# A graph stack of four attention layers: seven key blocks of the third layer turned by VectorE in the second, with masks fetched by quarters of the partitions

## The chip, the cores and the metric

The kernel runs on one core of a Trainium2 chip. The metric is the device time in microseconds from the start to the end of one execution; lower is better. The core has a matrix engine (TensorE, PE in the profile; its weight loads are PEld), a vector engine (VectorE, DVE), a scalar engine (ScalarE, ACT), GpSimd (POOL) and SyncE (SP), which here only issues transfers. GpSimd computes and issues transfers, both from one queue of instructions.

## The reference

Four graph attention layers over the same N = 4096 nodes and one adjacency matrix, D = 256 features. Each layer is followed by a residual sum and a layer norm. Cut to what matters:

```python
# layer 0: additive attention, 4 heads, softmax over j where adj; then elu
# layer 1: multi-head attention, 4 heads, scores q.k/8 + (adj.T - 1) * 10000
# layer 2: additive attention, one head
h = x @ W
e = leaky_relu((h @ a[:D])[:, None] + (h @ a[D:])[None, :], 0.01)
attention = softmax(where(adj > 0, e, -1e12), axis=1)
x = layernorm(x + elu(attention @ h))
# layer 3: cosine attention, rows of Wq x and Wk x normalised, mixed half and half with x
```

In the text they are called the first to the fourth layer. The change concerns how the third layer gets its operand `x @ W` and in which order it keeps the keys.

## The kernel before

The features X lie in SBUF for the whole run as 32 tiles of 128 nodes, `X[:, t, :]`. Every attention layer walks over 8 blocks of 512 queries (`NB`, `QW`), and inside a block over tiles of keys: 32 tiles of 128 in the first, third and fourth layer, 64 tiles of 64 in the second. One pair of block and key tile is called a unit. The layers follow one another at about 725, 1710 and 2213 us of the span.

*Second layer* (`multi_head_attention`, L536). Its main loop has an order written out by hand for TensorE, VectorE and ScalarE. A unit is: score matmuls (L664), an exponential on ScalarE (L666), the product with the mask on VectorE (L676), sums of the denominators on GpSimd (L683) and by accumulating transfers from GpSimd (L689), and the sums with V on TensorE (L697). `finish(b, j)` spreads the rest of a block over the units of the next: at step j of block b + 1 it joins denominators, turns results, and normalises rows of X; its last step was j = 41, when all four tiles of block b of X are final. For the last block, `tail` does this inside the third layer.

*Third layer* (`additive_one`, L401). A softmax weight factors into a term of the query (`src`) and a term of the key (`dst`), so a unit is one ScalarE instruction `e` (L456: relu of a row of query terms scaled by the key's), one VectorE instruction `prob` (L458: product with the mask) and four matmuls per query block into `acc` (L464, 8 records in the profile). Three buffers hold `prob`, four hold `mask`.

Before keys can be used, `x @ W` (`V`, with `src` and `dst` in its last columns) is made block by block: `turn(b)` transposes the four tiles of X on TensorE (`transposed_block`, 8 transposes at L118) and copies them out of PSUM on VectorE and ScalarE (L120); `project(b)` multiplies with W (L196), and ScalarE and VectorE write `src`, `dst` and `V` (L200 to L203). Blocks 0 and 1 are turned before the first unit; blocks 2 to 7 in the course of query block 0, `turn` at units 0, 4, ..., 20 and `project` two units later. After each `project`, `fill_row(b)` spreads `src` as a row over all partitions: for blocks 0 and 1 by TensorE (L446, L447), for the others by two transfers from GpSimd's queue, one to DRAM (`far`, L441) and one back to all partitions (`row`, L442), the second of which waits for the first at the head of the queue.

The order of TensorE in the third layer is written out by hand; a scheduler places the instructions of the other engines. The mask of two key tiles is one 512 KB transfer on SP's queue (L454), issued when the buffer is free.

*The end of the third layer.* `follow` (class `Cosine`) prepares the fourth layer within block 7 of the third: `prepare(b, step)` turns X by the other way. `turned_apart` (L123) makes two VectorE transposes of 32x32 squares (L131), stores the 512 KB in DRAM (`far`, L133) and fetches them by four 128 KB transfers, one for each quarter of 32 partitions (L135), so that a full turn comes out, with the keys of the block in another order. Step 0 does so for X on SP's queue, step 1 projects (L869) and normalises rows, step 2 turns these rows with `turned_apart` on GpSimd's queue (for six blocks) into `T`. GpSimd also fetches masks of the fourth layer (L854). L912 are the scores of the fourth layer, L920 its sums.

Of the kernel before, what the change touches and what calls it, by code (L numbers as in the profile page):

```python
# [9 lines left out]
FP = mybir.dt.float32  # L10
# [8 lines left out]
P = 128  # L19
D = 256  # L20
KC = D // P
QB = 4
QW = QB * P
# [5 lines left out]
def kernel(  # L29
# [49 lines left out]
    X = feat.tile([P, NT, D + 1], FP, name="X")  # L79
# [40 lines left out]
            copies[c](xT[:, c, :], pt)  # L120
        return xT.rearrange("p c (k i) -> p c k i", i=P)

    def turned_apart(squares, far, part, to, eng):  # L123

        B = P // QB
        squares = squares.tile([P, QB, KC, P], FP, name="squares")
        far = far.tile([QB, B, QB, KC * P], FP, name="far")
        for c in range(KC):  # L130
            nc.vector.transpose(squares[:, :, c, :].rearrange("p q (k n) -> p k q n", n=B),  # L131
                                part(c).rearrange("p k (q f) -> p k q f", f=B))
        eng.dma_start(far.rearrange("a f q m -> (a f) (q m)"), squares.rearrange("p q c m -> p (q c m)"))  # L133
        for q in range(QB):
            eng.dma_start(to[q * B:(q + 1) * B], far[:, :, q, :].rearrange("a f m -> f a m"))  # L135
        return to.rearrange("p a (c m) -> p c a m", c=KC)

    def block_apart(sb, once, dr, b, eng):
        xT = sb.tile([P, KC * QW], FP, name="xT").rearrange("p (a m) -> p a m", a=QB)
        return turned_apart(once, dr, lambda c: X[:, b * QB:(b + 1) * QB, c * P:(c + 1) * P], xT, eng)  # L140

    def one_row(mv, k, y):
        st = fin.tile([P, 6], FP, name="bn")
# [29 lines left out]
    def scale_row(y, mv, r, k):  # L173
        nc.vector.tensor_scalar(y, y, mv[:, k, 0:1], r[:, k:k + 1], OP.subtract, OP.mult)
# [226 lines left out]
    def additive_one(w_sb, slope, tail, op, follow):  # L401

        MJ = 2
        mvs, taken = {}, {}
        with ExitStack() as lay:
            keep = pool(lay, "gb_keep", 1)
            V = keep.tile([P, NT, D + 1], FP, name="V")
            src = keep.tile([P, NT, 1], FP, name="src")
# [1 line left out]
            row = keep.tile([P, N], FP, name="row")  # L410
            zp = pool(lay, "gb_z", 3)
            sb = pool(lay, "gb_sb", 2)
            xp = pool(lay, "gb_turn", 3)
            sq = pool(lay, "gb_squares", 1)
            far = pool(lay, "gb_far", 2, space=bass.MemoryType.DRAM)

# [2 lines left out]
            dr = pool(lay, "gb_dram", 2, space=bass.MemoryType.DRAM)  # L419

            ps = pool(lay, "gb_ps", 4, space=PSUM)
            pa = pool(lay, "gb_pa", 1, space=PSUM)
            edges = adjT.rearrange("(t p) i -> p t i", p=P)
            mask, acc, prob = {}, {}, {}

# [3 lines left out]
            def turn(b):  # L429
                return transposed_block(xp, bank, b)  # L430

            def project(b, xT, ks=range(QB)):
                groups = [(k, 1, bank().rearrange("p (n f) -> p n f", n=1)) for k in ks]
                additive_values(xT, b, groups, w_sb, V, src, dst, 1, slope)

            def fill_row(b):
                part = row[:, b * QW:(b + 1) * QW]
                if b > 1:

                    far = dr.tile([QB, P], FP, name="far")  # L440
                    nc.gpsimd.dma_start(far.rearrange("k p -> p k"), src[:, b * QB:(b + 1) * QB, 0])  # L441
                    nc.gpsimd.dma_start(part, far.rearrange("k p -> (k p)").unsqueeze(0).to_broadcast([P, QW]))  # L442
                    return
                pr = bank()
                for k in range(QB):
                    nc.tensor.transpose(pr[:, k * P:(k + 1) * P], src[:, b * QB + k, :].to_broadcast([P, P]), ident)  # L446
                nc.scalar.copy(part, pr)  # L447

            def weights(b, j):
                cols = slice(b * QW, (b + 1) * QW)  # L450
                m = b, j // MJ
                if j % MJ == 0:
                    mask[m] = mp.tile([P, MJ, QW], I32, name="mask")
                    nc.sync.dma_start(mask[m], edges[:, j:j + MJ, cols])  # L454
                e = sb.tile([P, QW], FP, name="e")
                nc.scalar.activation(e, row[:, cols], AF.Relu, bias=-1.0, scale=dst[:, j, :])  # L456
                prob[b, j] = zp.tile([P, QW], FP, name="prob")
                nc.vector.scalar_tensor_tensor(prob[b, j], e, 1.0, mask[m][:, j % MJ, :], OP.add, OP.mult)  # L458
# [26 lines left out]
            even = itertools.count()  # L485
            units = [(b, j) for b in range(NB) for j in range(NT)]
            with tc.manual_schedule(engines={mybir.EngineType.PE}):
                xTs = {0: turn(0), 1: turn(1)}
                project(0, xTs[0])
                project(1, xTs[1], [0, 1])  # L490
                fill_row(0)
                project(1, xTs[1], [2, 3])
                for i in range(len(units) + 1):
                    if i < len(units):
                        b, j = units[i]
                        weights(b, j)

                        if b == 0 and j // QB + 2 < NB:
                            n = j // QB + 2
                            if j % QB == 0:  # L500
                                xTs[n] = turn(n)
                            elif j % QB == 2:
                                project(n, xTs[n])
                                fill_row(n)
                    if i:
                        b, j = units[i - 1]
                        sums(b, j)
                        if (b, j) == (0, 1):
# [27 lines left out]
    def multi_head_attention(w_sb, b_sb, tail, rows_of_den, narrow_edges):  # L536
# [8 lines left out]
        MJ = 4  # L545
# [3 lines left out]
        with ExitStack() as lay:  # L549
# [91 lines left out]

            zp = pool(lay, "mh_z", 8)
            mp = pool(lay, "mh_mask", 3)
            ps = pool(lay, "mh_pz", 3, space=PSUM)
            pa = pool(lay, "mh_pa", 1, space=PSUM)
            mask, acc, prob, score = {}, {}, {}, {}
# [112 lines left out]
            def finish(b, j):  # L759

                rows = [X[:, b * QB + k, :D] for k in range(QB)]
                if j in (7, 9):
                    join_sums(b, j // 2 - 2)
                elif j == 12:
                    row_sums(halves(), b)
                elif j == 15:
                    bank = halves()
                    pd = turned_row_sums(bank, b)
                    po = turned_half(bank, b, 0)
                    reciprocals(pd, b)  # L770
                    half(po, b, 0)
                elif j == 18:
                    half(turned_half(halves(), b, 2), b, 2)
                elif j in (21, 23, 25, 27):
                    k = (j - 21) // 2
                    if k == 0:
                        mvs[b] = fin.tile([P, QB, 2], FP, name="mv")
                    one_row(mvs[b], k, rows[k])
                elif j == 29:
                    roots[b] = begin_root(mvs[b])  # L780
                elif j == 31:

                    end_root(*roots[b], nc.gpsimd)
                elif j in (35, 37, 39, 41):
                    k = (j - 35) // 2
                    scale_row(rows[k], mvs[b], roots[b][1], k)

# [40 lines left out]
    class Cosine:  # L828

        MJ = 4  # L830
# [192 lines left out]
        return part[:, t:t + QB, :]  # L1023

    w2_sb = const.tile([P, KC, D + 2], FP, name="w2_sb")
    wm_sb, bm_sb = {}, {}
    with ExitStack() as weights1, ExitStack() as den1, ExitStack() as weights3:
        wp = weights1.enter_context(tc.tile_pool(name="w1", bufs=1, side="right"))
# [66 lines left out]
```

## Time and profile before

The times of three runs and the profiled execution:

| | us |
|---|---|
| median of three runs | 2892.49 (2891.81 to 2894.18) |
| profiled execution | 2892.62 |
| its span | 2890.8 |
| TensorE busy in the span | 2879.6 |
| third layer on TensorE | 1710.2 to 2212.9 |
| its query block 0 | 1710.2 to 1803.8 |
| its query block 7 | 2136.9 to 2212.9 |

The granted clock of TensorE was 0.999 of full speed over the span. GpSimd's groups in the third layer's block 0, with mean durations of one instruction:

| group | instructions | mean ns |
|---|---|---|
| L441 `far<-src`, POOL issue | 6 | 775 |
| L442 `row<-far`, POOL issue | 6 | 546 |
| L706 denominators of the last block, POOL | 2 | 2601 |

How to read it: a row of a timeline is a run of like instructions on one engine, with its start and length, and in brackets the idle time before it and what ended it. The length of a matmul includes its way through the pipeline, so rows overlap a little; the difference of two starts is what a group costs. A transfer's issue on an engine's queue is short; when it lands is another matter, and an instruction that waits for the landing holds up its whole queue.

### The profile page before, as it was taken

Reading aid. Unit: us, or ns where it says so; the run is one execution under the profiler, and the core shown is the slowest. Engines: PE = TensorE matmul, PEld = TensorE weight load, DVE = VectorE, ACT = ScalarE, POOL = GpSimd, SP = SyncE. Lnnn points to the kernel's source line nnn. Section 1 sums busy time; section 2 is a strip of 40 time slices with the busy share of each in tenths; the row PEclk is TensorE's granted clock in tenths of the full one; section 3 lists DMA queues with packets and bytes.
Section 4 is the critical chain, followed back from the end, with each engine's and each line's share of the span. In section 5 each row is a group of like instructions: output and inputs, shape, how many; then the busy total and the mean of one; then the engine's idle time right before and its main releaser. Section 6 shows DMA issues by size and latency. Waiting matters only on the chain.

```text
span 2890.8 us, 50566 instructions
## 1 busy us (share of the span) xinstructions
PE 2879.6 (100%) x20093; PEld 1548.7 (54%) x20093; DVE 1959.5 (68%) x2557; ACT 1652.8 (57%) x2582; POOL 945.9 (33%) x705
## 2 busy tenths in 40 slices
PE   9999999999999999999999999999999999999999
PEld 4333333333543333333333358888888777777776
DVE  8899999998777777777777765655667323333333
ACT  7899999997356666666666653444444222222222
POOL 0010010100068988989899870000002000000000
PEclk9999999999999999999999999999999999999999
DMA  7566667675269989889899885565566434333441
GB/s 206 103 139 137 142 134 145 138 133 92 88 138 192 183 187 196 181 187 190 182 193 188 181 178 133 164 184 158 159 185 178 76 57 58 59 58 59 59 59 30
DMA packets 237087, 398.04 MB, mean 138 GB/s; under 512 B 20929, under 2 KB 121265, under 8 KB 235954
## 3 DMA queue, kind: packets, MB, share of 16 engines
q0 software_dynamic: 104320, 184.06, 40.1%
q1 hardware_dynamic: 132112, 210.36, 23.7%
q8 instruction: 157, 2.57, 0.3%
q14 instruction: 80, 0.66, 0.1%
q10 hardware_dynamic: 418, 0.40, 0.0%
HBM read 328.60 MB, written 32.58 MB: 125 GB/s over the span
## 4 chain that ended last, share of the span: by engine, by line
PE 99%; DVE 1%; ACT 0%; DMA 0%; issue 0%; SPq 0%; DVEq 0%
PE acc L293 23%; PE acc L920 15%; PE acc L697 15%; PE p L664 15%; PE acc L464 8%; PE g L464 8%; PE p L912 4%; PE g L912 3%; PE g L579 2%; PE g L196 1%; PE pv L598 1%; PE acc L869 1%; PE acc L196 1%; PE g L118 1%; PE g L305 0%; PE p L734 0%
## 5 line engine op out<-in xcount | busy, mean ns | idle before, releaser
L676 DVE TENSOR_TENSOR prob<-p,mask 128x1024 f32<-128x1024 f32 x512 | 624.0, 1223 | 209.4 <-ACT p L666 203.6
L666 ACT ACTIVATE p<-p,shift 128x1024 f32<-128x1024 f32 x512 | 556.2, 1088 | 325.2 <-PE p L664 324.4
L293 PE MATMUL acc<-prob,V 128*32 128x512 f32 x6144 | 664.0, 593 | 1.1 <-DVE prob L283 1.1
L683 POOL TENSOR_TENSOR den<-den,prob 128x1024 f32<-128x1024 f32 x248 | 626.4, 2526 | 73.9 <-DVE prob L676 66.6
L280 ACT ACTIVATE prob<-row,dst 128x512 f32<-128x512 f32 x1020 | 633.1, 712 | 0.1
L283 DVE SCALAR_TENSOR_TENSOR prob<-prob,mask 128x2048 f32<-128x2048 f32 x256 | 582.7, 2287 | 24.2 <-ACT prob L280 21.3
L664 PE MATMUL p<-qT,kT 64*64 64x512 f32 x4096 | 532.7, 590 | 0.8 <-DVE prob L676 0.8
L697 PE MATMUL acc<-prob,V 64*64 64x512 f32 x4096 | 531.8, 590 | 0.0
L920 PE MATMUL acc<-X,prob 128*128 128x257 f32 x2048 | 485.4, 380 | 0.0
L920 PEld LDWEIGHTS acc<-X,prob 128*128 128x128 f32 x2048 | 389.2, 190 | 161.6 <-issue 112.3
L917 DVE TENSOR_TENSOR prob<-prob,mask 128x512 f32<-128x512 f32 x256 | 176.7, 690 | 405.6 <-ACT prob L916 405.4
L293 PEld LDWEIGHTS acc<-prob,V 128*32 128x32 f32 x6144 | 197.8, 110 | 452.6 <-issue 431.9
L91 POOL COPY tick<-prob 128x1 f32<-128x1 f32 x35 | 40.2, 1150 | 996.0 <-DVE prob L283 644.5
L456 ACT ACTIVATE e<-row,dst 128x512 f32<-128x512 f32 x256 | 184.1, 721 | 241.7 <-DVE prob L458 212.7
L697 PEld LDWEIGHTS acc<-prob,V 64*64 64x64 f32 x4096 | 156.0, 133 | 285.2 <-issue 277.9
L664 PEld LDWEIGHTS p<-qT,kT 64*64 64x64 f32 x4096 | 154.6, 133 | 277.2 <-issue 261.4
L458 DVE SCALAR_TENSOR_TENSOR prob<-e,mask 128x512 f32<-128x512 f32 x256 | 175.5, 686 | 169.8 <-PE acc L464 92.4
L854 POOL DMA_DIRECT2D mask<-in_adjT x64 | 48.1, 751 | 585.2 <-DVE prob L917 523.6
L689 POOL DMA_DIRECT2D den<-prob x240 | 233.2, 972 | 15.7 <-DVE prob L676 6.7
L916 ACT ACTIVATE prob<-p 128x512 f32<-128x512 f32 x144 | 85.7, 596 | 258.4 <-PE p L912 244.3
L464 PE MATMUL acc<-V,prob 128*128 128x257 f32 x1024 | 225.1, 380 | 0.0
L464 PE MATMUL g<-V,prob 128*128 128x257 f32 x1024 | 223.7, 380 | 0.0
(165 smaller groups left out, 1937.1 us busy)
## 6 DMA issues: line engine op xcount, KB each, us to landing
mask<-in_adjT SPq DMA_DIRECT2D x256, 512.0 KB
den<-prob POOLq DMA_DIRECT2D x240, 512.0 KB, 5.1
mask<-edges SPq DMA_DIRECT2D x512, 64.0 KB
mask<-in_adjT POOLq DMA_DIRECT2D x64, 512.0 KB, 5.7
edges<-in_adj POOLq DMA_DIRECT2D x32, 512.0 KB, 9.8
far<-squares SPq DMA_DIRECT2D x16, 512.0 KB
den<-prob SPq DMA_DIRECT2D x16, 512.0 KB
row<-far SPq DMA_DIRECT2D x7, 1024.0 KB
```

The source lines that it names most:

```text
L280: nc.scalar.activation(z[:, h, :], r, AF.Relu, bias=-1.0, scale=dst[:, j, h:h + 1])
L283: nc.vector.scalar_tensor_tensor(z, z, 1.0, mask[m][:, j % MJ, :].unsqueeze(1).to_broadcast([P, H, QW]), OP.add, OP.mult)
L293: nc.tensor.matmul(acc[b][h * G:(h + 1) * G, n, :], part, prob[b, j][:, h, :], start=(j == 0), stop=(j == NT - 1))
L464: nc.tensor.matmul(acc[b][k][:, :D + 1], prob[b, j][:, k * P:(k + 1) * P], V[:, j, :], start=(j == 0), stop=(j == NT - 1))
L664: nc.tensor.matmul(p[c * d:(c + 1) * d, r, :], kT[half, c, at:at + d], qT[half, c, cols], start=True, stop=True)
L666: nc.scalar.activation(p, p, AF.Exp, bias=shift)
L676: nc.vector.tensor_tensor(z, p, mask[m][:, j % MJ, :].unsqueeze(1).to_broadcast([P, KC, QW]), OP.mult)
L683: nc.gpsimd.tensor_tensor(to, to, flat, OP.add)
L689: nc.gpsimd.dma_start(to, flat, accum_op=OP.add)
L697: nc.tensor.matmul(acc[b][c][r * d:(r + 1) * d, :], V[half, j, r * d:(r + 1) * d], prob[b, j][half, r, :], start=(j == 0), stop=(j == NH - 1))
L912: nc.tensor.matmul(p.rearrange("p (k i) -> p k i", k=QB), T[j // QB][:, 0, j % QB], T[b][:, 1], start=True, stop=True)
L920: nc.tensor.matmul(acc[b][k], prob[b, j][:, k * P:(k + 1) * P], X[:, j, :], start=(j == 0), stop=(j == NT - 1))
```

## The change

In the second layer, `finish` gets a step at j = 44: `squares_of` transposes the 32x32 squares of block b of X on VectorE (two instructions) and stores them in DRAM on SP's queue, for b = 0 to 6. In the third layer `fetch(b)` takes the place of `turn(b)` for these seven blocks: four transfers on SP's queue bring the squares to `xT`. Block 7, which is final only inside the third layer, is still turned by TensorE. Three blocks are fetched ahead instead of two turned.

The keys of a turned block come out in another order: key tile a of the block holds the nodes k x 128 + a x 32 + n. The masks of these tiles are therefore fetched in four quarters of 32 partitions, through the view `apart`; in query block 0 all four on SP's queue, in later blocks quarters 1 and 3 on GpSimd's. `fill_row` brings the row of query terms back into the order of the nodes: for blocks 0 and 1 in ScalarE's copy, for blocks 2 to 6 by four transfers to DRAM instead of one. The pool of `xT` is set up first in the layer, so that its buffers lie where the second layer's `kT` lay.

```diff
-    def turned_apart(squares, far, part, to, eng):
+    def squares_of(squares, far, part, eng):
...
         eng.dma_start(far.rearrange("a f q m -> (a f) (q m)"), squares.rearrange("p q c m -> p (q c m)"))
+        return far
+
+    def squares_placed(far, to, eng):
+        B = P // QB
         for q in range(QB):
             eng.dma_start(to[q * B:(q + 1) * B], far[:, :, q, :].rearrange("a f m -> f a m"))
         return to.rearrange("p a (c m) -> p c a m", c=KC)
...
         with ExitStack() as lay:
+
+            xp = pool(lay, "gb_turn", 3)
             keep = pool(lay, "gb_keep", 1)
...
-            xp = pool(lay, "gb_turn", 3)
...
+            apart = adjT.rearrange("(b k a n) i -> k n b a i", k=QB, a=QB, n=P // QB)
             edges = adjT.rearrange("(t p) i -> p t i", p=P)
...
+            def fetch(b):
+                return squares_placed(turned[b], new_xT(xp), nc.sync)
...
-                    far = dr.tile([QB, P], FP, name="far")
-                    nc.gpsimd.dma_start(far.rearrange("k p -> p k"), src[:, b * QB:(b + 1) * QB, 0])
-                    nc.gpsimd.dma_start(part, far.rearrange("k p -> (k p)").unsqueeze(0).to_broadcast([P, QW]))
+                    far = dr.tile([QB, QB, P // QB], FP, name="far")
+                    if b < NB - 1:
+                        for k in range(QB):
+                            at = slice(k * P // QB, (k + 1) * P // QB)
+                            nc.gpsimd.dma_start(far[k].rearrange("a n -> n a"), src[at, b * QB:(b + 1) * QB, 0])
+                    else:
+                        nc.gpsimd.dma_start(far.rearrange("k a n -> (a n) k"), src[:, b * QB:(b + 1) * QB, 0])
+                    nc.gpsimd.dma_start(part, far.rearrange("k a n -> (k a n)").unsqueeze(0).to_broadcast([P, QW]))
...
-                nc.scalar.copy(part, pr)
+                nc.scalar.copy(part.rearrange("p (k a n) -> p a k n", k=QB, a=QB),
+                               pr.rearrange("p (a k n) -> p a k n", k=QB, a=QB))
...
-                    nc.sync.dma_start(mask[m], edges[:, j:j + MJ, cols])
+                    if j // QB in turned:
+
+                        for k in range(QB):
+
+                            eng = nc.gpsimd if b and k % 2 else nc.sync
+                            eng.dma_start(mask[m][k * P // QB:(k + 1) * P // QB],
+                                          apart[k, :, j // QB, j % QB:j % QB + MJ, cols])
+                    else:
+                        nc.sync.dma_start(mask[m], edges[:, j:j + MJ, cols])
...
-                xTs = {0: turn(0), 1: turn(1)}
+                xTs = {0: fetch(0), 1: fetch(1)}
+                xTs[2] = fetch(2)
...
-                            if j % QB == 0:
+                            if j % QB == 0 and n + 1 in turned:
+                                xTs[n + 1] = fetch(n + 1)
+                            elif j % QB == 0 and n + 1 == NB:
                                 xTs[n] = turn(n)
...
+            sq = pool(lay, "mh_squares", 1)
...
+                elif j == 44:
+                    turned[b] = squares_of(sq, turned_far, chunk(b), nc.sync)
...
+    turned = {}
+    turned_far = ctx.enter_context(tc.tile_pool(name="turned", bufs=NB - 1, space=bass.MemoryType.DRAM))
```

More of the change, by code (lines that the diff above doesn't have):

```diff
@@ L136, in turned_apart, with chunk, new_xT @@
         return to.rearrange("p a (c m) -> p c a m", c=KC)
+    def turned_apart(squares, far, part, to, eng):
+        return squares_placed(squares_of(squares, far, part, eng), to, eng)
+    def chunk(b):
+        return lambda c: X[:, b * QB:(b + 1) * QB, c * P:(c + 1) * P]
+    def new_xT(sb):
+        return sb.tile([P, KC * QW], FP, name="xT").rearrange("p (a m) -> p a m", a=QB)
     def block_apart(sb, once, dr, b, eng):
-        xT = sb.tile([P, KC * QW], FP, name="xT").rearrange("p (a m) -> p a m", a=QB)
-        return turned_apart(once, dr, lambda c: X[:, b * QB:(b + 1) * QB, c * P:(c + 1) * P], xT, eng)
+        return turned_apart(once, dr, chunk(b), new_xT(sb), eng)
     def one_row(mv, k, y):
```

## The prediction

> **What bounds the kernel now.** I read the busy table and the chain of waits first, then TensorE's timeline around the start of the third layer, then the waits and GpSimd's timeline there and at the layer's end.
>
> ```profile
> PE 2879.6 (100%) x20093; PEld 1548.7 (54%) x20093; DVE 1959.5 (68%) x2557; ACT 1652.8 (57%) x2582; POOL 945.9 (33%) x705
> ...
> PE 99%; DVE 1%; ACT 0%; DMA 0%; issue 0%; SPq 0%; DVEq 0%
> ```
>
> TensorE (PE) has work for 2879.6 of 2890.8 us at full clock. So TensorE work that goes is worth its whole duration, and any edit that leaves TensorE waiting costs its whole wait: there is no other slack to take. Next, the timeline of TensorE where layer 3 begins (columns: start, duration, engine, line, operation, count; ends overlap, so I take differences of starts).
>
> ```profile
> 1707.41 2.87 PE L697 MATMUL acc<-prob,V 64*64 64x512 f32 x22
> 1710.21 1.97 PE L118 MATMUL g<-ident,X 128*128 128x128 f32 x16
> 1712.01 5.39 PE L196 MATMUL g<-w_sb,xT 128*128 128x258 f32 x24
> 1717.25 0.60 PE L446 MATMUL g<-ident,src 128*128 128x128 f32 x4
> 1717.68 1.91 PE L196 MATMUL g<-w_sb,xT 128*128 128x258 f32 x8
> 1719.43 1.03 PE L118 MATMUL g<-ident,X 128*128 128x128 f32 x8
> 1720.30 1.90 PE L464 MATMUL acc<-V,prob 128*128 128x257 f32 x8
> ...
> 1729.43 1.04 PE L118 MATMUL g<-ident,X 128*128 128x128 f32 x8
> ```
>
> No idle time is printed behind any row. Two turned blocks (16 transposes) take 1712.01 - 1710.21 = 1.80 us and one takes 1720.30 - 1719.43 = 0.87. One key tile of sums (8 records of L464) takes 1.735. Further turns start at 1742.83, 1754.13, 1765.43 and 1776.72; the last is block 7, which stays.
>
> Then the waits of that stretch (1710 to 1804), the timelines of GpSimd and of VectorE and TensorE in the layer's last block, the DMA share there (last but one column), and the landing times of the 128 KB transfers that GpSimd issues there.
>
> ```profile
> POOL row L442 <- DMA far<-src: 36.0, 4, 10.3
> ```
> ```profile
> 2171.16 2.20 POOL L135 DMA_DIRECT2D T<-far  x4 [7.96 <-DMA far<-squares]
> 2173.35 0.57 POOL L133 DMA_DIRECT2D far<-squares  x1
> 2173.91 0.20 POOL L91 COPY tick<-prob 128x1 f32<-128x1 f32 x1
> 2174.03 1.51 POOL L854 DMA_DIRECT2D mask<-in_adjT  x2
> 2179.58 2.21 POOL L135 DMA_DIRECT2D T<-far  x4 [4.04 <-DMA far<-squares]
> ```
> ```profile
> 2178.66 0.68 DVE L458 SCALAR_TENSOR_TENSOR prob<-e,mask 128x512 f32<-128x512 f32 x1
> ```
> ```profile
> 2176.55 7.10 PE L464 MATMUL g<-V,prob 128*128 128x257 f32 x32
> 2183.48 3.62 PE L869 MATMUL acc<-w_sb,xT 128*128 128x256 f32 x16
> ```
> ```profile
> 2150.00:2190.00 40.00, 40.00 (x187) 35.14 (x186) 28.86 (x62) 21.63 (x89) 11.91 (x21) 1.00 1.07 262
> ```
> ```profile
> DMA to landing us min/median/max: 2.8/4.5/8.2
> ```
>
> The reader should see that GpSimd's queue is not busy but blocked: it stands at its head up to 10.3 us for one transfer and 4 to 8 us for each `far`, and everything issued behind it stands too. Today nothing that TensorE needs soon is behind it. The DMA engines are full in that stretch (share 1.07).
>
> **What the Trainium skill says.** "DMA: Bandwidth & Descriptors", section "Issuing engines are not separate DMA queues": transfers from sync, scalar and gpsimd run on the same 16 DMA engines and interleave. So a second queue gives no bandwidth; that the full stretch above mixes transfers of both queues agrees. The same page, "Rules for kernel authors", advises against cutting one transfer by partitions; no quartered mask is in the trace before. Its "Anatomy of one DMA" fit for gpsimd, 2.0 us + bytes/436e3, gives an estimate of 2.3 us for 128 KB; the trace has 2.8 at least and 4.5 in the median, and I use the trace. "VectorE: DVE Perf Modes", "The three transpose paths": VectorE turns only 32x32 blocks, so a full turn needs the pieces moved too, as the squares are here.
>
> **The change part by part** (minus is gained).
>
> *Layer 2: two VectorE transposes and a 512 KB store per block, at step 44 of 64.* L131 takes 0.70 us at this shape, so 2 x 0.70 = 1.4 us in one go. VectorE is busy 1.223 us per 1.72 us unit (L676). The nearest row is the join at L706, 1.21 us, which stands between L676 rows at 938.73 and again at 942.15: the score matmuls (L664) start at 938.73, 940.45 and 942.16, one unit apart, so it cost nothing. The eight `prob` buffers and three score banks cover about 1.6 us. The store goes to SP while the DMA share is 0.91; masks there are fetched three buffers ahead. Cost 0; ends 0 and +2.5 (7 x 0.35, a partial stall in each block). It can't be below 0, as TensorE loses nothing there.
>
> *Start of layer 3.* 16 transposes (1.80) go. In their place the first fetch on SP waits for the buffer's last reader, the last score matmul near 1706.7, issues four DMAs to about 1708.3, and must land. Such a round on SP took 2.6 to 3.6 us in the second layer's prologue, so 1711.7 with 1711 to 1713 as ends: `project(0)` starts at 1711.7 and not 1712.01, so the wait on transfers gives back most of the 1.80. The third turn (0.87 at 1719.43) goes too, but VectorE now does all eight V products (L203, 0.43 us) before prob(0,0) (0.69 us) and not six. The last projection ends near 1719.1; V, then prob bring 1719.1 + 0.2 + 2 x 0.43 + 0.69, about 1720.9, for sums(0,0), which started at 1720.30. Net +0.6 (-0.9 to +2).
>
> *Four turns later in block 0.* 4 x 0.87 = -3.5. PSUM copies L120 go with them, off the path. Block 0 in sum: -2.9 (-4.4 to -1.5).
>
> *Masks of block 0, in quarters, all on SP.* SP issues a DMA in about 0.43 us. Behind 12 fetches, with eight transfers in flight on a queue, the first mask lands near 1715 and the second near 1722; needed 1719 and 1726. Cost 0 (0 to +1), held in the start's ends.
>
> *fill_row for blocks 2 to 7.* For blocks 2 to 6 four issues at 0.55 replace one at 0.76: 5 x 1.4 = +7 us on GpSimd. The idle time between its fills is 0.7 to 2.2, in sum 6.1, so the last row goes out about where it did (1796.5), to 1 us later. New: the first masks of block 1 have two quarters on this queue and stand behind it. Issued 1797.5 to 1798.6, landing 2.8 to 4.5 later: 1801.4 to 1803.1; wanted near 1800.2 (1803.8 less 2.9 less 0.69). Four transfers of 128 elements may land sooner than one of 512 (8.3 to 10.8 us), which takes several us off the chain. I take +1.0, ends 0 and +5.
>
> *Blocks 1 to 6.* Half the mask is on an otherwise empty GpSimd queue (it was busy 0.00 from 1804 to 2137), 1.1 us of issues per 3.5 us, four mask buffers ahead. Nothing to wait for: 0.
>
> *Block 7.* In the built order the second GpSimd quarter of the mask for tiles 18 and 19 stands behind the four T DMAs of block 2, which wait at the head of the queue for `far` (the row at 2179.58). So it issues at 2179.58 + 2.21 = 2181.8, lands at +4.5 to +5.7 (the medians of T and of the 512 KB masks from GpSimd in this stretch), and prob 18 follows in 0.68: 2187.0 to 2188.2. TensorE wants tile 18 at 2176.55 + 3 x 1.735 = 2181.75. Stall +5.9 (+3.5 at the fastest landing, 2.8; +9 at the slowest, 8.2). Before, prob 18 was at 2178.66 with its mask long there. The same happens to tiles 22 and 23 (both quarters behind T of block 3) and 26 (behind T of block 4): VectorE does the squares of 3 and 4 earlier in the new order and the first stall moves the need, so these cost +0.9 and +3.5 by the same steps. Against it: five score matmuls of layer 4 (L912, about 0.86 each) now stand ahead of sums(7,26) and fill that last stall, and their prob products are done early, while at 2212.94 to 2215.75 layer 4 waits now: -3.3. Net +7.0 (+2 to +12).
>
> Sum: 0 - 2.9 + 1.0 + 0 + 7.0 = +5.1 us. The profiled execution takes 2890.8 + 1.82 outside the span = 2892.62, 0.13 above the median of 2892.49; on the median I forecast 2892.5 + 5.1, rounded to 2898. Below 0.2% (5.8 us) I call a change none: about what a measurement of this kernel can tell.
>
> **The rivals.**
> *A, the transposes go and nothing replaces them* (faster). The place is `far` at the head of GpSimd's queue in block 7. It landed 6.2 us after its issue (2173.35 to 2179.58), 3.0 at the fastest in this layer. Where it lands in about 2.7 and the mask quarter in 2.8, prob 18 is in time and the block stalls nowhere; from that point block 0's -2.9 to -4.4 stands alone with some -2 of the early layer-4 scores: 2886 to 2888, say 2887. Against it: the order of the queue is a fact of the built program, and the DMA engines are full there.
> *B, the two halves cancel* (no change): the waits for tiles 22 and 26 are swallowed by the first, TensorE fills the last with layer 4's scores; +2 in block 7, 2892 to 2894. For it: three prob buffers and the shifted need.
> *C, the software queue decides everywhere* (slower still): the fills of the row run at 12 us each and block 1 waits 5 us, landings in the full stretch go to 8 us and more, since half of the mask bytes are now on the queue that was slow there, and layer 2 pays 2.5: -2 + 5 + 12 + 2.5, about 2910. For it: landings up to 11.3 us of masks from GpSimd between 2140 and 2180; against: these are 512 KB each.
>
> **How the numbers follow.** My case (block 7 stalls three times, net +2 to +10, 2894 to 2904) 0.52; A 0.16; B 0.20; C 0.12. The time is my case's, 2898. Range 2888 to 2907: from most of A to the near side of C, leaving out about 2 in 10. Of my case about 0.38 lies above 2898.3 and 0.14 below; with C slower is 0.50. Of A, 0.10 passes 5.8 us and 0.06 does not; with B, same is 0.40. Faster 0.10.
>
> **What would show it.** In the new trace: no L118 in layer 3 but 8; project(0) near 1711.7, kept waiting by a transfer; idle time of TensorE before tile 18 of block 7, released by prob, whose own wait ends with a mask quarter from GpSimd; block 1's first tile late by about 1 us; matmul spacing in layer 2 unchanged. I am wrong if block 7 runs without gaps (A), if the gap sits at block 1 or in the start, or if the layer-2 units beside step 44 are longer than 1.72 us.

## The result, and where the time went

The changed kernel takes 2914.95 us (median of four, 2911.06 to 2915.88) against 2892.15 for the kernel before (four runs, 2891.78 to 2894.18): 22.8 us longer, a ratio of 1.0075 with a 95% interval of 1.0061 to 1.0089. The forecast was 2898, with a range that ended at 2907. The profiled execution is the fastest of the four: span 2909.3, 18.5 us over the span before.

The busy row and the chain of waits of the page, after:

```profile
PE 2878.9 (99%) x20037; PEld 1542.5 (53%) x20037; DVE 1963.6 (67%) x2564; ACT 1649.2 (57%) x2575; POOL 1058.7 (36%) x916
...
PE 97%; DVE 1%; DMA 1%; ACT 0%; issue 0%; SPq 0%; POOL 0%; DVEq 0%; POOLq 0%; ACTq 0%
```

TensorE executes 56 matmuls fewer (20037 against 20093), yet its busy time fell by 0.7 us and not by 6: some of the rest ran more slowly. And it now waits. Every wait of TensorE in the third layer stands in its timeline with a bracket (lines of the changed kernel: L208 is the projection, L495 the sums, L489 `prob`, L906 the projection for the fourth layer, L949 its scores):

```profile
1705.40 3.73 PE L732 MATMUL acc<-prob,V 64*64 64x512 f32 x32
1713.07 7.16 PE L208 MATMUL g<-w_sb,xT 128*128 128x258 f32 x24 [3.93 <-DMA xT<-far]
1720.06 0.60 PE L468 MATMUL g<-ident,src 128*128 128x128 f32 x4
1720.50 1.91 PE L208 MATMUL g<-w_sb,xT 128*128 128x258 f32 x8
1726.28 2.00 PE L495 MATMUL acc<-V,prob 128*128 128x257 f32 x8 [3.87 <-DVE prob L489]
...
1750.72 7.16 PE L495 MATMUL acc<-V,prob 128*128 128x257 f32 x24 [4.26 <-DVE prob L489]
...
2195.92 3.40 PE L495 MATMUL g<-V,prob 128*128 128x257 f32 x8 [5.20 <-DVE prob L489]
...
2209.34 2.00 PE L495 MATMUL g<-V,prob 128*128 128x257 f32 x8 [1.35 <-DVE prob L489]
...
2225.12 10.68 PE L495 MATMUL g<-V,prob 128*128 128x257 f32 x48 [0.63 <-DVE prob L489]
```

The waits sum to 19.2 us. Note the lengths too: the same 24 projections took 5.39 us before and take 7.16 after the first wait. The windows show the granted clock (last but two columns) and the DMA share (last but one):

```profile
1705.00:1709.00 4.00, 4.00 (x40) 1.10 (x32) 2.45 (x2) 1.11 (x2) 3.83 (x3) 1.00 0.93 198
1713.00:1717.00 4.00, 3.93 (x12) 3.20 (x13) 0.85 (x2) 0.59 (x6) 2.26 (x2) 0.64 1.14 218
```

After the wait the clock is 0.64 of full speed for 4 us. From the stages on TensorE in both profiled executions the account can be closed (the sign is after less before; a sum counts as over 0.17 us before the printed end of its row, since rows overlap by that much):

| stretch of TensorE's time | before | after | difference | forecast |
|---|---|---|---|---|
| span's start to the end of the second layer's last sum | 1710.11 | 1708.96 | -1.15 | 0 |
| from there to the third layer's first sum | 10.19 | 17.32 | +7.13 | +0.6 |
| rest of query block 0 | 83.34 | 86.17 | +2.83 | -3.5, and +1.0 at its end |
| blocks 1 to 6 | 333.08 | 333.08 | 0.00 | 0 |
| block 7 and the fourth layer | 754.08 | 763.77 | +9.69 | +7.0 |

The first row isn't the second layer. Its blocks take 896.98 us before (813.13 to 1710.11) and 896.97 after (811.99 to 1708.96). The difference arises in the first microseconds of the span, where twelve matmuls of the first projection took 3.75 us before, 2.92 after and up to 5.30 in other profiled runs. In the profiles of all runs the second layer's main loop begins between 811.99 us (after) and 815.57 (e2_turn01), so up to 3.6 us of a single profile are chance of the start.

### The profile page after: what moved, and what is told of

Read it like the earlier page. It is cut to its first block, busy times and chain, and to the rows that moved or that the text cites. A ratio compares the mean times of both kernels' runs of the same rounds, so it can differ in the third digit from the quotient of the medians.

```text
span 2909.3 us, 51372 instructions
## 1 busy us (share of the span) xinstructions
PE 2878.9 (99%) x20037; PEld 1542.5 (53%) x20037; DVE 1963.6 (67%) x2564; ACT 1649.2 (57%) x2575; POOL 1058.7 (36%) x916
## 4 chain that ended last, share of the span: by engine, by line
PE 97%; DVE 1%; DMA 1%; ACT 0%; issue 0%; SPq 0%; POOL 0%; DVEq 0%; POOLq 0%; ACTq 0%
PE acc L305 23%; PE acc L957 15%; PE p L699 15%; PE acc L732 15%; PE acc L495 8%; PE g L495 7%; PE p L949 4%; PE g L949 3%; PE g L613 2%; PE g L208 1%; PE pv L632 1%; PE acc L208 1%; DMA mask<-in_adjT 1%; PE acc L906 0%; PE g L317 0%; PE g L118 0%
## 5 line engine op out<-in xcount | busy, mean ns | idle before, releaser
L489 DVE SCALAR_TENSOR_TENSOR prob<-e,mask 128x512 f32<-128x512 f32 x256 | 176.4, 692 | 161.3 <-PE acc L495 75.5
L724 POOL DMA_DIRECT2D den<-prob x240 | 232.6, 969 | 18.5 <-DMA den<-prob 7.1
L495 PE MATMUL acc<-V,prob 128*128 128x257 f32 x1024 | 226.3, 382 | 8.1 <-DVE prob L489 8.1
L495 PE MATMUL g<-V,prob 128*128 128x257 f32 x1024 | 225.9, 382 | 7.2 <-DVE prob L489 7.2
```

The lines of the kernel that those rows point to most:

```text
L495: nc.tensor.matmul(acc[b][k][:, :D + 1], prob[b, j][:, k * P:(k + 1) * P], V[:, j, :], start=(j == 0), stop=(j == NT - 1))
L724: nc.gpsimd.dma_start(to, flat, accum_op=OP.add)
```

## The experiments

My theory after this reading had four parts. The first fetches land late because the DMA engines are still full with the second layer's last transfers. VectorE's order in block 0, placed by the scheduler, has changed, and causes the wait of 4.26 us. In block 7 mask quarters stand behind the blocked GpSimd queue, as forecast. And long waits are paid twice, by a slow clock after them. Rivals: the masks are late whichever queue brings them; twelve fetches in a row hold each other up; the late first `prob` is a mask's fault.

**Masks on SP alone.**

```diff
-                            eng = nc.gpsimd if b and k % 2 else nc.sync
+                            eng = nc.sync
```

> One edit to the changed kernel: all four quarters of every mask go on SP's queue in every block. If the quarters behind the blocked GpSimd queue cause block 7's stalls, those (5.20 + 1.35 + 0.63 us) and the slow clock after the first (about 1.8 us) go: 2904 to 2907 against 2915. If the quarters are late because the DMA engines are full there, whatever queue issues them, the stalls stay: 2913 to 2916. The start of the layer (11.9 us of waits) is the same in both.

Measured: 2982.68 us, ratio 1.0312 (1.0297 to 1.0327), 68 us over the changed kernel and far from both expectations. Each of blocks 1 to 6 now has two waits near its start (2.25 and 3.0 us); block 7 begins with one of 12.63 us and then waits 4.8 us about every 17. VectorE's timeline at the start of block 1 shows why:

```profile
1817.74 1.29 DVE L489 SCALAR_TENSOR_TENSOR prob<-e,mask 128x512 f32<-128x512 f32 x2
1818.94 0.42 DVE L225 TENSOR_TENSOR X<-X,o 128x256 f32<-128x256 f32 x1
...
1823.27 1.38 DVE L186 TENSOR_SCALAR X<-X,mv,r 128x256 f32<-128x256 f32 x4
1824.57 1.28 DVE L489 SCALAR_TENSOR_TENSOR prob<-e,mask 128x512 f32<-128x512 f32 x2
```

VectorE works almost without idle time (0.57 us) through the outputs of block 0, and the next pair of `prob` stands behind them. No mask is late here. The edit changed the order that the scheduler gave VectorE, so the run says nothing of the queue itself. It says that in a kernel like this one a transfer's queue is also an input of the scheduler: the built order has to be read again for every variant. (Why the scheduler places them so was not examined.)

**Blocks 0 and 1 turned by TensorE again**, their masks whole and their rows copied plainly.

```diff
-                xTs = {0: fetch(0), 1: fetch(1)}
+                xTs = {0: turn(0), 1: turn(1)}
...
-                elif j == 44:
+                elif j == 44 and b > 1:
```

> Blocks 0 and 1 are turned by TensorE again (16 transposes, 1.80 us), with their masks whole; blocks 2 to 6 stay as in the changed kernel. If the fetches at the layer's start (and the first mask that stands behind twelve of them) cause the waits of 3.93 and 3.87 us and the slow clock after, those go, and the one of 4.26 us in part (VectorE's order there moves too): about -10 to -13, 2902 to 2905. If the start's loss has another cause (VectorE locked out, the order alone), less than half of this goes: 2909 to 2914. Block 7 stalls as before the edit.

Measured: 2899.72 us, ratio 1.0024 (1.0015 to 1.0033), 15.2 us less than the changed kernel. From the second layer's last sum to the first sum of the third it takes 9.90 us, less than before the change (10.19); the rest of block 0 takes 81.09 (before 83.34). Both stretches are now gains, with waits of 0.41 and 0.85 left. Block 7 loses as before the edit (a wait of 4.32, then 1.35). The gain is a little over the 10 to 13 us expected; a likely reason is that the wait of 4.26 us, of which a part was expected to stay, went almost whole and its slow clock with it.

**Both edits together.**

> Both edits together: blocks 0 and 1 turned by TensorE, all mask quarters on SP. If the two causes are independent and are all there is, the sum of both gains: near 2893, and down to 2888 (2892.2 less five turns of 0.87) where nothing of the stalls is left. If a third cause holds (the order of VectorE's work in block 0, or the fill of the row on GpSimd), it stays above 2895.

Measured: 2908.47 us (ratio 1.0055, 1.0040 to 1.0070), 8.7 over e2_turn01. Blocks 1 to 6 have no waits here, block 7 has five, two of them of 4.82 us, with VectorE's squares directly ahead of the `prob` that TensorE waits for and no mask late, as in block 7 of e1_masks_sp.

**One sum on GpSimd left out.** In the profile after, the first `prob` of the layer starts beside GpSimd's second sum of denominators (L741):

```profile
1723.34 2.33 POOL L741 TENSOR_TENSOR den<-den 128x1024 f32<-128x1024 f32 x1 [8.08 <-DMA den<-prob]
```
```profile
1723.67 3.15 DVE L489 SCALAR_TENSOR_TENSOR prob<-e,mask 128x512 f32<-128x512 f32 x2 [0.21 <-DMA mask<-in_adjT]
```
```profile
L489 DVE SCALAR_TENSOR_TENSOR prob<-e,mask x256: 646/691/2548, 1723.7 to 2230.7; 128x512 f32<-128x512 f32 x128
```

The two `prob` together take 3.15 us, and one of all 256 (the last line: minimum, median, maximum) took 2548 ns where the median is 691.

```diff
-                join_sums(b, 2, nc.gpsimd)
```

> The changed kernel without the second GpSimd sum of the last block's denominators (it leaves out a third of that block's denominator), which lies beside prob(0,0), a VectorE instruction of 2.55 us where the others take 0.68. If GpSimd's sum locks VectorE out of its memory port, prob(0,0) takes 0.68 and the first sums start about 1.9 us sooner: 2912 to 2913.5. If prob(0,0) was slow for another reason (its mask landing), no change: 2914.5 to 2915.5.

Measured: 2912.27 us (2911.26 to 2913.57; ratio 1.0067, 1.0050 to 1.0084). The two take 1.28 us, and the wait of TensorE before its first sum falls from 3.87 to 1.71. In the profiles of e6_fetch2_late and e7_tail7, where the start lies some 1 us otherwise and the sum is not left out, `prob` came first. There the pair takes 1.28 as well and it is GpSimd that pays:

```profile
1726.50 2.87 POOL L740 TENSOR_TENSOR den<-den 128x1024 f32<-128x1024 f32 x1 [8.21 <-DMA den<-prob]
```

In these profiles whoever starts second takes longer. The Trainium skill says this in "SBUF — State Buffer", section "Who interferes with whom": a VectorE instruction with two SBUF inputs and a GpSimd instruction that reads SBUF share a port pair, and the second to issue fully blocks. The trace agrees: 1723.34 + 2.33 is 1725.67, the `prob` ended 0.55 us later. In the kernel before, the first `prob` was long over when the sum began at 1722.77; it met the fourth, which had started 0.07 us earlier, and there the sum took 2.84 us and that `prob` 0.69.

**Block 7: the two queues swapped**, on top of e2_turn01. All mask quarters go on GpSimd, squares and T on SP.

```diff
-                            eng = nc.gpsimd if b and k % 2 else nc.sync
+                            eng = nc.gpsimd if b == NB - 1 or b and k % 2 else nc.sync
...
-                             nc.gpsimd if b < NB - 2 else nc.sync)
+                             nc.sync)
```

> Blocks 0 and 1 turned by TensorE, and in block 7 the queues are swapped: all mask quarters on GpSimd's queue, the transfers of squares and T on SP's. The built order of VectorE has probs 18 and 22 ahead of the squares again. If the blocked queue is what holds block 7's masks, its waits of 4.32 and 1.35 us and the slow clock after the first go: 2899.7 less 6 to 9, 2890 to 2894. If the full DMA engines are (any queue lands late there), or SP's turn to stand blocked holds up something else, 2897 or more.

Measured: 2894.14 us, ratio 1.0007 (0.9999 to 1.0016): 5.6 less than e2_turn01 and just above the 2890 to 2894 of the first reading. One wait of 1.92 us is left in block 7; VectorE waits up to 3.64 us for a `far` to land before it may write the next squares into the only buffer, and later `prob` stand behind: SP's turn to stand blocked costs something too.

**Each fetch one step later**, in the changed kernel: eight transfers and not twelve before the first mask.

```diff
-                xTs[2] = fetch(2)
...
-                            if j % QB == 0 and n + 1 in turned:
-                                xTs[n + 1] = fetch(n + 1)
+                            if j % QB == 0 and n in turned:
+                                xTs[n] = fetch(n)
```

> The changed kernel with the third block's fetch (and each later one) issued one step later, so that eight fetches and not twelve stand ahead of the first mask. If the first fetch lands late because twelve transfers of 128 KB share the DMA engines with the second layer's last sums, project(0) starts 1 to 3 us sooner and the first mask, prob(0,0) and the sums with it; VectorE also gets probs 6 and 7 ahead of the last block's halves, so the wait of 4.26 us and its slow clock go in part: 2905 to 2911. If the first landing is latency alone, project(0) stays at 4 us of wait and only the order helps: 2909 to 2912.

Measured: 2911.41 us (ratio 1.0067, 1.0051 to 1.0084). TensorE waits 4.79 us for the first fetch, no less than with twelve. So the last four of the twelve do not hold up the first; whether the first eight hold each other up was not tested. In this profile two later waits are shorter: 2.26 us in block 0 instead of 4.26, where two more `prob` stand ahead of the last block's halves, and 1.71 before the first sum instead of 3.87, since `prob` came before GpSimd's sum. How the gain of 3.5 us divides between them was not measured.

**The tail's last step two units later**, in the changed kernel. The rows of VectorE's timeline, first of the kernel before, then of the changed kernel, show the order around this step (L742 and L777 are its first instruction):

```profile
1736.49 0.77 DVE L203 TENSOR_TENSOR V<-g,V 128x256 f32<-128x256 f32 x2 [0.97 <-PE g L196]
...
1739.99 0.69 DVE L458 SCALAR_TENSOR_TENSOR prob<-e,mask 128x512 f32<-128x512 f32 x1 [0.98 <-PE acc L464]
1740.60 0.27 DVE L742 RECIPROCAL rden<-g 128x8 f32<-128x8 f32 x2
```
```profile
1735.21 1.30 DVE L489 SCALAR_TENSOR_TENSOR prob<-e,mask 128x512 f32<-128x512 f32 x2 [1.46 <-ACT e L487]
1741.17 0.42 DVE L215 TENSOR_TENSOR V<-g,V 128x256 f32<-128x256 f32 x1 [4.66 <-ACT V L214]
...
1745.63 0.28 DVE L777 RECIPROCAL rden<-g 128x8 f32<-128x8 f32 x2 [1.42 <-PE g L762]
...
1749.99 0.68 DVE L489 SCALAR_TENSOR_TENSOR prob<-e,mask 128x512 f32<-128x512 f32 x1
```

Before, nine `prob` (tiles 0 to 8) stand ahead of L742. After, only six do: VectorE stands 4.66 us idle at the head of its queue, waiting for a projection, while the seventh `prob`, whose operands are there, stands behind it and behind the whole step. (ScalarE had finished its `e` by 1739.95, and the last quarter of its mask had been issued at 1730.09, 11 us before.)

```diff
-                        if b == 0 and j in (0, 3, 5):
-                            tail(bank, (0, 3, 5).index(j))
-                            if j == 5:
+                        if b == 0 and j in (0, 3, 7):
+                            tail(bank, (0, 3, 7).index(j))
+                            if j == 7:
```

> The changed kernel with the last step of the second layer's tail two units later (after sums 7 and not 5), which puts probs 6, 7 and 8 ahead of that step in VectorE's order; nothing else moves. If VectorE's order is the cause of the third stall (4.26 us, and about 1.8 of slow clock after it), it goes: 2908 to 2910. If the mask of tiles 6 and 7 is late, the stall stays near where it was: 2913 to 2916.

Measured: 2909.81 us (ratio 1.0059, 1.0044 to 1.0074), 5.1 less. The wait of 4.26 is replaced by one of 1.81 four tiles later, without slow clock, and the rest of block 0 takes 82.04 us where it took 86.17. TensorE's part of the step moves along with it, so the stretch was not changed in VectorE's order alone; but no mask was issued sooner, and the tiles after the old place run without a wait. The order was the cause.

**Three edits together** (turn01, swap7, tail7).

> Together: blocks 0 and 1 turned by TensorE, the swap of queues in block 7, the tail's last step two units later. If these are all the causes, what is left is the five turns saved (4.35 us) less small waits: 2888 to 2891, faster than the kernel before. If a cause is missing, 2893 or more.

Measured: 2895.25 us, ratio 1.0010 (1.0003 to 1.0016), no better than e5_swap7. With blocks 0 and 1 turned on TensorE the old place of the step was already good (a wait of 0.85); two units later it costs 1.94, and block 7 waits 0.89, 0.59 and 1.91 in this profile. A repair fits the order that it was found for.

**Block 7: quarters 1 and 3 on ScalarE's queue**, on top of e2_turn01.

```diff
-                            eng = nc.gpsimd if b and k % 2 else nc.sync
+                            eng = (nc.scalar if b == NB - 1 else nc.gpsimd) if b and k % 2 else nc.sync
```

> Blocks 0 and 1 turned by TensorE; in block 7 quarters 1 and 3 of the masks go on ScalarE's queue, T and squares stay on GpSimd's. Then no mask quarter stands behind a blocked instruction, and VectorE's built order in block 7 has every prob ahead of the squares as in the kernel before. If the blocked queue and VectorE's order are the whole cause of block 7's loss, its waits go and what is left is the five turns saved: 2888 to 2891. If the quarters land late for the full DMA engines, or ScalarE loses by issuing, 2893 or more.

> The same kernel as e9_act7, timed once more, since its interval reached just to no change: 2889 to 2892 against 2892 for the kernel before if its gain of five turns (4.35 us less waits of 0.4 and 0.9 at the layer's start) is real; an interval across 1.000 again if it can't be told apart.

Measured: 2890.74 us (13 runs) against 2892.48, ratio 0.9993 (0.9984 to 1.0001), and again 2890.28 against 2892.39, ratio 0.9993 (0.9985 to 1.0001). It is 9.0 us below e2_turn01, from which it differs by this line. TensorE in block 7, and the issues of these quarters on ScalarE's queue (minimum, median and maximum in ns):

```profile
2174.22 7.10 PE L494 MATMUL g<-V,prob 128*128 128x257 f32 x32
2181.16 3.62 PE L905 MATMUL acc<-w_sb,xT 128*128 128x256 f32 x16
2184.62 7.10 PE L494 MATMUL g<-V,prob 128*128 128x257 f32 x32
```
```profile
L481 ACTq DMA_DIRECT2D mask<-in_adjT x14: 317/318/367, 2151.2 to 2188.8; - x14
```

The waits of 4.32 and 1.35 us are gone; one of 0.19 is left (0.55 in the second profile). Block 7 up to the fourth layer's first sum takes 79.55 us (before 79.03, changed 92.92). The built order of VectorE in block 7 also changed, back to every `prob` ahead of the squares, so the run takes away both at once, and its 9.0 us can't be divided between them. It is the best version found. It is 1.7 and 2.1 us below the kernel before in two series, but each interval ends just above 1, so no more than "not slower, probably faster by less than 0.1%" is shown.

**The last transfers of the second layer left out**, in the changed kernel.

```diff
-                else:
+                elif b < NB - 1 or j < NH - 10:
                     to = den[b][:, 1 + j // 2 % 2, :]
```

> The changed kernel without the last five accumulating transfers of denominators at the second layer's end (part of the last block's denominator is left out), so that GpSimd's queue sends nothing to the DMA engines while the first blocks are fetched. If those full DMA engines hold up the first fetch (7.4 us from the first issue to project(0), where such a round took 2.6 to 3.6 us in the second layer's prologue), TensorE's wait at the layer's start falls from 4 to 5 us to 2 or less and the slow clock after it goes. If the twelve fetches of 128 KB hold each other up, or the landing is latency, the wait stays at 4 us.

Measured: 2907.31 us in a single run. TensorE at the layer's start, and the DMA share before it (in the changed kernel the second of these stretches had 0.93):

```profile
1711.06 5.48 PE L208 MATMUL g<-w_sb,xT 128*128 128x258 f32 x24 [1.07 <-DMA xT<-far]
```
```profile
1700.00:1705.00 5.00, 5.00 (x52) 1.72 (x48) 3.59 (x4) 3.11 (x4) 3.47 (x2) 1.00 0.00 0
1705.00:1709.00 4.00, 4.00 (x44) 1.29 (x40) 2.86 (x3) 1.95 (x2) 2.91 (x2) 1.00 0.33 94
```

The first issue stands at 1706.49 and the projection starts 4.6 us later, where the changed kernel took 7.4 (1705.64 to 1713.07); the projections run at full clock (5.48 us for 24). The twelve fetches are the same in both, so most of the late landing comes with the second layer's last accumulating transfers, and latency alone is ruled out, as far as a single run shows. At the start of block 1 a wait of 1.60 us and one of 0.81 appear: before the first, a `prob` waits 4.63 us for a mask quarter that GpSimd issued behind its fills of the row.

**The price of a wait**, measured in the kernel before.

```diff
+                if 0 < b < NB - 1 and j in (21, 29):
+                    for _ in range(2 * b + (j == 29) + 4):
+                        nc.vector.tensor_scalar(prob[b, j], prob[b, j], 1.0, 0.0, OP.mult, OP.add)
```

> The kernel before, with a chain of 6 to 17 VectorE instructions that multiply one prob tile by 1 at twelve places in blocks 1 to 6, so that TensorE waits for different lengths (about 0 to 7 us) where nothing else changes. If a wait of TensorE longer than a threshold near 3.9 us is followed by a stretch of slow clock, the matmuls after each longer wait take 1.5 to 3 us more than the same number after a shorter one, which take 1.735 us a tile. If the 1.8 us after the waits of the changed kernel came from something else (late weights, late probs), the pace after every wait is the same.

Measured in a single run of 2953.26 us, in TensorE's timeline (64 matmuls are eight tiles, 24 are three):

```profile
1964.12 14.15 PE L467 MATMUL g<-V,prob 128*128 128x257 f32 x64 [2.95 <-DVE prob L461]
1981.68 5.47 PE L467 MATMUL g<-V,prob 128*128 128x257 f32 x24 [3.42 <-DVE prob L461]
...
2027.45 15.83 PE L467 MATMUL acc<-V,prob 128*128 128x257 f32 x64 [3.88 <-DVE prob L461]
2047.62 7.16 PE L467 MATMUL acc<-V,prob 128*128 128x257 f32 x24 [4.33 <-DVE prob L461]
...
2188.93 8.49 PE L467 MATMUL acc<-V,prob 128*128 128x257 f32 x24 [6.18 <-DVE prob L461]
```

The waits came out at 0.63, 1.56, 2.03, 2.49, 2.95, 3.42, 3.88, 4.33, 4.80, 5.26, 5.72 and 6.18 us. After the six longest the next matmuls took 1.4 to 3.0 us more; after those of 2.49 to 3.42 none. But the one of 2.03 was followed by 15.83 us too, with the clock at 0.57 in its first 4 us, and in the changed kernel the wait of 3.87 was not. So below some 4 us the length of a wait does not decide; the last section shows what does. The slow stretch comes from the wait: only the VectorE chains were added to a kernel that has none there.

## Why the prediction was wrong, step by step

*Right.* Layer 2 costs nothing (896.97 us), blocks 1 to 6 cost nothing (333.08), and block 7's first and longest stall has the reason given. GpSimd's timeline of the changed kernel has the quarter behind T, and VectorE, done with its squares, waits for it:

```profile
2188.40 2.20 POOL L139 DMA_DIRECT2D T<-far  x4 [4.59 <-DMA far<-squares]
2190.60 0.55 POOL L482 DMA_DIRECT2D mask<-in_adjT  x1
```
```profile
2190.14 1.30 DVE L131 STREAM_TRANSPOSE squares<-rows 128x512 f32<-128x512 f32 x2
2195.18 1.29 DVE L489 SCALAR_TENSOR_TENSOR prob<-e,mask 128x512 f32<-128x512 f32 x2 [3.73 <-DMA mask<-in_adjT]
```

Issued at 2190.60, it had landed by 2195.18, 4.6 us later; VectorE waits 3.73 us for it with nothing else to do, so the mask and not VectorE's order ended this stall. The second stall, of 1.35 us, is another matter. Its `prob` does not wait for a mask; it stands behind VectorE's squares for the fourth layer:

```profile
2207.40 1.31 DVE L131 STREAM_TRANSPOSE squares<-rows 128x512 f32<-128x512 f32 x2
2208.63 1.25 DVE L489 SCALAR_TENSOR_TENSOR prob<-e,mask 128x512 f32<-128x512 f32 x2
```

The waits of 5.20, 1.35 and 0.63 make 7.2 us. The forecast had 5.9, 0.9 and 3.5, less 3.3 that score matmuls of the fourth layer would fill; ten records of them, the five of the forecast, did stand ahead of the third wait. (That step also says that the fourth layer waits at 2212.94 to 2215.75 in the kernel before. TensorE does not wait there, it runs six of these records; what they save is that they fill a stall.) The net of +9.7 against +7.0 holds about 1.5 us of slow clock after the first wait, which the step lacked; about 1 us is not accounted for. In the third stall `prob` stands behind squares again; VectorE had come to them late, after 5.64 us of waiting for the mask of tiles 24 and 25, and how much of this stall that explains was not measured. So the size was near and the first stall was understood, but a late mask as the cause of the second was wrong.

*Wrong: "Start of layer 3".* The step put project(0) at 1711.7, "such a round on SP took 2.6 to 3.6 us in the second layer's prologue", and the net at +0.6. It took +7.1. First, the landing was priced from a stretch where the DMA engines are busy 0.26 of the time (725 to 806 us) and used where they are busy 0.93 (0.87 at the same place, 1705 to 1709 us, in the kernel before). This is worth 2.5 us (a wait of 4.1 and not 1.6); in e10_no_last_den, without the last transfers, the wait is 1.07. Second, the slow clock after it, +1.8, which no step of the prediction counts. Third, the first sum: the sum of the step said that V and `prob` keep TensorE waiting 1.8 us after the last projection. Without GpSimd's sum beside it this is 1.71 us, as said; with it 3.87, 2.2 more. The three make 6.5, the gap between forecast and measurement.

*Wrong: "Four turns later in block 0".* The step counted 4 x 0.87 = -3.5 and took VectorE's order in this block as it was. The turns did go, but the wait of 4.26 us and its slow clock of 1.8 came: +2.8. This order could be read from the built program before any run. The forecast looked at the order on GpSimd and SP and, for VectorE, at the first V products and at block 7 only.

*The sizes of fill_row.* The cost of +1.0 at block 1 did not appear in the changed kernel, probably because everything ahead was 9 us late and gave GpSimd time; that is luck. Waits do appear at block 1 in e10_no_last_den (2.4 us), e4_no_join (0.81) and e7_tail7 (0.50).

*The rivals.* Rivals A and B fell with block 7, which loses 9.7 us net. Rival C gave 2910, for landings of 8 us in block 7 and late masks in block 1. The time is nearer to it, its mechanism is not what happened: the late quarter of tile 18 landed in 4.6 us, and block 1 did not wait.

*What stays open.* The profile shows 18.5 us, the medians differ by 22.8. No profile of a 2915 us run was taken. The mean granted clock of each run is on record: 0.998 in the profiled one, 0.996, 0.996 and 0.995 in the other three. A difference of 0.002 over 2909 us is 5.8 us of full clock, about what these runs take longer (3.3 to 4.8 us), so longer or more slow stretches are the likely reason. Which waits set them off was not profiled; in the variants with the same start and end the first wait lies between 3.9 and 4.8 us and the one in block 7 between 4.6 and 5.8. It is also open why e2_turn01, e3_turn01_masks_sp and e5_swap7 show an idle 1.3 us at the first layer's first projection where most others show 0.3.

## What to carry to other kernels

Price a transfer's landing from a stretch of the trace whose DMA share is that of the place where it will be issued, not from where the same transfer happens to be seen. When an edit changes queues or sizes of transfers and a scheduler places an engine's instructions, read the new order of that engine in every stage beside what bounds the kernel: here an in-order queue that stood at an instruction not yet ready cost more than any of the edit's own instructions. And where TensorE is at 100%, add to every wait of some 4 us or more the slow restart, 1.4 to 3 us here, and keep it as a risk for waits of 2 to 4 us.

## What the runs showed of the hardware

In the profiled runs of this study every TensorE wait of 3.88 us or more in the third layer was followed by 1.4 to 3.0 us of lost pace. Of the shorter ones two were (2.03 in e11_gaps, 2.26 in e6_fetch2_late), while others up to 3.87 went free.

The clock records of the profiles tell them apart. From the second layer to shortly before the end of a run the granted clock is 1.00 or 0.50. Each stretch at 0.50 lasts 3.41 us or a whole multiple of it, and within a run all of them begin on one grid of such steps, wherever the waits lie. Nine profiles have slow stretches in the third layer. When TensorE's idle time there is counted step by step, each of the 30 full-clock steps with 2.03 us of it or more is followed by a step at half clock, and none of the 86 steps with 0.3 to 1.95 us is. In e11_gaps the wait of 2.03 us lay in one step whole (the first number after the comma is TensorE's busy time):

```profile
1898.12:1901.53 3.41, 1.38 (x7) 0.90 (x6) 2.67 (x7) 1.45 (x2) 0.00 (x0) 1.00 0.35 115
1901.53:1904.94 3.41, 3.41 (x10) 2.67 (x9) 0.63 (x1) 0.00 (x0) 0.00 (x0) 0.50 0.37 130
```

The wait of 3.87 us in the changed kernel was split between two steps, 1.94 and 1.93 us, and went free. So a wait under 2 us went free wherever it fell, one over some 4 us has at least 2 us in one step, and for those between, the place on the grid decides. A step at half clock, full of matmuls, costs half of 3.41, about 1.7 us; less where part of the step falls into the wait.

The Trainium skill describes the clock gate in "TensorE: Matmul & The Clock Gate", "Part 1: The HAM clock gate": after an idle window of about 3.4 us the clock is halved, until a busy window of the same length has passed. The trace agrees in the length of the step. It differs in what counts as idle: here 2.03 us of idle time in a step of 3.41 were enough.

The block of GpSimd and VectorE on each other was a surprise in its price on the path: a single `prob` of 2.55 us instead of 0.69, in a kernel where GpSimd's share is a third, and only where it starts within the 2.3 us of the sum.
